# Seven block products in place of eight for values, feed-forward base and output projection of a gated attention block

## Chip, cores and metric

The kernel runs on one core of a Trainium2 chip. Its time is the device time in microseconds from launch to end, the median of several runs. The engines of a core work beside each other, each through its own queue in order: TensorE (PE in the profile; its weight loads PEld), VectorE (DVE), ScalarE (ACT), GpSimd (POOL), and SyncE (SP), which here issues nearly all transfers.

## Reference

Two batches of 1024 tokens with 512 features, all in fp32. D is 512, 32 heads of 16, 8 experts of rank 16 with the best 2 chosen.

```python
xn = layernorm(x)
q, k, v = xn @ Wq.T + bq, xn @ Wk.T + bk, xn @ Wv.T + bv
att = softmax(where(causal, q @ k.T / 4, -inf))       # per head
s = (att @ v) @ Wo.T + bo
base = xn @ W_base.T + b_base
route = top-2 of softmax(xn @ W_gate.T), normalized
delta = ((xn @ A.T) * route) @ B
g = silu(base + delta * SCALING)
out = x + s * g
```

## The kernel before

The work is cut into chunks (b, c) of 512 tokens, two batches by two chunks. Attention runs over *units* (b, oc, c): eight heads (oc) of one chunk. Each unit is a list of *steps*; 144 steps in all stand in `plan`. In a step n, TensorE computes the scores of four heads for 512 columns (`scores`, L923, tile `s`), ScalarE takes their exponential in two halves (L932, tile `pt`), VectorE multiplies the causal part by a mask (`masked`, L951; 83 of the 144 steps have one), and in the following step TensorE multiplies by the values (`values`, L967, tile `av`). The order in each engine's queue is: scores of step n, values of step n-1, masks of step n, then `fill(n)`.

`fill` is a planner that runs while the program is built. It holds every other piece of TensorE work as a `Task`, a generator that emits a piece and says what it cost. The unit of cost is `MM`, 0.853 us by the planner's own figure, for one group of eight matmuls with 512 columns (an fp32 matmul of a 128 by 128 block is issued as four strips of 32 columns, each in two passes). A task has a due step, an earliest step (`after`), buffers that it takes and frees (`room`), and a condition (`ready`). In each step the planner emits the ready tasks in order of due step, until the step has had its even share of what is left; work that is due is emitted whatever the share. Tasks without cost (layernorm, routing, loads) advance once in each step until they say `WAIT`. A list `later` holds the pieces of the softmax normalization that follow a unit by two to seven steps: the sums of the exponentials go to DRAM (`den`), come back spread over partitions (`dens`), their reciprocals go out (`back`) and in again (`avs`), all on SP's queue.

Three projections are the ones that the change touches. Each takes the normalized and transposed tokens `xnT` (or the attention output `oT`) as the matmul's left operand, 128 tokens at a time, and a weight that lies whole in SBUF (`wv_sb`, `wb_sb`, `wo_sb`, 1 MB each) as the right:

- values: `v_task` (L394), four groups a tile of 128 tokens, one VectorE addition of the bias (L402), into a tile of 17 columns a head;
- gate: `gate_task` (L498), four groups for the base and one more for the routed part in the same PSUM tile, one VectorE addition (L508), then tanh on ScalarE (L511) and two GpSimd operations (L512, L513);
- output: `out_task` (L598), four groups a tile, a VectorE addition (L607), two GpSimd operations (L608, L609) and the store. Each tile's x is loaded again (`load_x`, L88).

So a chunk costs 16 groups in each of the three, and 4 more for the routed part. The last chunk's output, at the end of the kernel, goes another way: `most_task`, `whole_task` and `rest_task` follow the last unit tile by tile, with x loaded by `bases_task` (L621) eight to nine steps before the end.

PSUM has two tiles for all of these projections (`ps_mm`), two for the scores and two for the attention output. `room` counts the SBUF buffers: one x chunk, three `xnT`, twelve `v` tiles, eight `g` tiles.

The transfers that matter in the order of SP's queue: a fill's own loads and stores as its tasks emit them, then what `later` emits, then those of tasks without cost. A transfer that has to wait for its operand keeps all behind it on that queue waiting.

Of the kernel before, what the change touches and what calls it, by code (L numbers as in the profile page):

```python
# [17 lines left out]
P = 128  # L18
# [41 lines left out]
def direct(ctx, tc, sound, x, wq, wk, wv, wo, wb, wa, wg, wB, bq, bk, bv, bo, bb, out):  # L60
# [22 lines left out]
    ps_av = ctx.enter_context(tc.tile_pool(name="ps_av", bufs=2, space=PSUM))  # L83


    def load_x(b, i):
        xt = sb.tile([P, D], F32, tag="xr", name=f"xr_{b}_{i}")
        nc.sync.dma_start(out=xt, in_=x[b, i * P : (i + 1) * P, :])  # L88
        return xt

    def chunk_tile(b, c):
        return sb.tile([P, TT, D], F32, tag="x", bufs=1, name=f"x_{b}_{c}")

# [5 lines left out]
    def load_w(src, cols, name, o0=0):  # L99
# [3 lines left out]
        )  # L103
        return t

    def load_b(src, name):
        t = cst.tile([P, D], F32, name=name)
        nc.sync.dma_start(out=t, in_=src.partition_broadcast(P))
        return t
# [3 lines left out]
    nc.scalar.dma_start(out=b_rows[KC : 2 * KC], in_=bk.rearrange("(kc p) -> kc p", p=P))  # L113
    wq_sb = [load_w(wq, P, "wq_sb0")]
    wk_sb = [load_w(wk, P, "wk_sb0")]
    wv_sb = load_w(wv, D, "wv_sb")
    bv_sb = load_b(bv, "bv_sb")
    for oc in range(1, KC):
        wq_sb.append(load_w(wq, P, f"wq_sb{oc}", oc * P))
        wk_sb.append(load_w(wk, P, f"wk_sb{oc}", oc * P))  # L120
    wag_sb = cst.tile([P, KC, ER + E], F32, name="wag_sb")
    wb_sb = cst.tile([P, KC, D], F32, name="wb_sb")
    wB_sb = cst.tile([P, D], F32, name="wB_sb")
    bb_sb = cst.tile([P, D], F32, name="bb_sb")
    wo_sb = cst.tile([P, KC, D], F32, name="wo_sb")
    bo_sb = cst.tile([P, D], F32, name="bo_sb")

    def load_rest():


        def by_rows(w):
            return w.rearrange("(kc p) o -> p kc o", p=P)

        for dst, src in (
            (wag_sb[:, :, 0:ER], by_rows(wa)),
            (wag_sb[:, :, ER:], by_rows(wg)),
            (wb_sb, by_rows(wb)),
            (wB_sb, wB),
            (bb_sb, bb.partition_broadcast(P)),
            (wo_sb, by_rows(wo)),  # L140
            (bo_sb, bo.partition_broadcast(P)),
        ):
            nc.sync.dma_start(out=dst, in_=src)
# [48 lines left out]
    def mm_tile(name):  # L192
        return ps_mm.tile([P, D], F32, tag="mm", name=name)
# [187 lines left out]
    def project(ps, b, i, w, stop=True):  # L381
        xnT, t = xnTs[b, i // TT], i % TT
        for k in range(KC):
# [7 lines left out]
            if k < KC - 1:  # L391
                yield

    def v_task(b, i):  # L394
        pv = mm_tile("pv")
        for _ in project(pv, b, i, wv_sb):
            yield MM
        v = sb.tile([P, VW], F32, tag="v", bufs=12, name=f"v_{b}_{i}")
        vh = v[:, 0 : H * VS].rearrange("p (h r) -> p h r", h=H)
        nc.gpsimd.memset(vh[:, :, HD : HD + 1], 1.0)  # L400
        nc.gpsimd.memset(v[:, H * VS : VW], 0.0)
        nc.vector.tensor_add(  # L402
            vh[:, :, 0:HD],
            pv.rearrange("p (h r) -> p h r", h=H),
            bv_sb.rearrange("p (h r) -> p h r", h=H),
        )
        vs[b, i] = v
        yield MM

    def routed_task(b, c):  # L410

# [83 lines left out]
        hls[b, c] = hl  # L495
        projected_at[b, c] = now[0]

    def gate_task(b, i):  # L498

        pb = mm_tile("pb")  # L500
        for _ in project(pb, b, i, wb_sb, stop=False):
            yield MM
        yield MM
        matmul(
            pb, lhsT=hwTs[b, i // TT][:, :, i % TT], rhs=wB_sb, start=False, stop=True
        )
        gt = sb.tile([P, D], F32, tag="g", bufs=8, name=f"g_{b}_{i}")
        nc.vector.tensor_add(gt, pb, bb_sb)  # L508

        sg = sb.tile([P, D], F32, tag="tmp", name="sg")  # L510
        nc.scalar.activation(sg, gt, AF.Tanh, scale=0.5)  # L511
        nc.gpsimd.tensor_scalar(sg, sg, 0.5, 0.5, ALU.mult, ALU.add)  # L512
        nc.gpsimd.tensor_tensor(gt, gt, sg, ALU.mult)  # L513
        gs[b, i] = gt
        yield MM

    def outputs(b, c):
        if (b, c) not in oTs:
            oTs[b, c] = sb.tile([P, KC, C], F32, tag="oT", name=f"oT_{b}_{c}")
# [69 lines left out]
    def project_out(po, b, c, t, k0, k1):  # L589
        for k in range(k0, k1):  # L590
            matmul(
                po, lhsT=oTs[b, c][:, k, t * P : t * P + P], rhs=wo_sb[:, k, :],
                start=k == k0, stop=k == k1 - 1,
            )
            if k < k1 - 1:
                yield

    def out_task(b, c):  # L598

        for t in range(TT):  # L600
            i = c * TT + t
            xt = load_x(b, i)
            po = mm_tile("po")
            for _ in project_out(po, b, c, t, 0, KC):
                yield MM
            y = sb.tile([P, D], F32, tag="tmp", name="y")
            nc.vector.tensor_add(y, po, bo_sb)  # L607
            nc.gpsimd.tensor_tensor(y, y, gs.pop((b, i)), ALU.mult)  # L608
            nc.gpsimd.tensor_tensor(y, y, xt, ALU.add)  # L609
            nc.sync.dma_start(out=out[b, i * P : (i + 1) * P, :], in_=y)  # L610
            yield MM

    def turn_last(b, c, t, turned):
        pt = mm_tile("pt_y")[:, 0:P]
# [1 line left out]
        nc.scalar.copy(oTs[b, c][:, KC - 1, t * P : t * P + P], pt)  # L616
        turned.append(t)

    bases = {}

    def bases_task(b, c):  # L621

        xt = chunk_tile(b, c)
        nc.sync.dma_start(
            out=xt, in_=x[b, c * C : (c + 1) * C].rearrange("(t p) d -> p t d", p=P)
        )
        for t in range(TT):
            bases[t] = xt[:, t]
        yield 0.0

    def finish_tile(b, c, t, po):
# [34 lines left out]
    def rest_task(b, c, t):  # L666

        turned = []
        last_in_range()
        yield lambda: turn_last(b, c, t, turned), TR  # L670
        while not turned:
            yield WAIT
        po = mm_tile("po")
        matmul(
            po, lhsT=oTs[b, c][:, KC - 1, t * P : t * P + P], rhs=wo_sb[:, KC - 1],
            start=True, stop=True,
        )
        pn = mm_tile("pn")[0:1, 0:NF]
        nc.tensor.matmul(pn, lhsT=ones, rhs=fine, start=True, stop=True)
        finish_tile(b, c, t, po)  # L680
        count = small.tile([1, 1], F32, tag="count", bufs=1, name="count")
        nc.vector.tensor_reduce(count, pn, AX.X, ALU.add)
        nc.vector.tensor_copy(sound, count)
        yield MM
# [54 lines left out]
        plan += [(u, s, n == 0, n == len(steps) - 1) for n, s in enumerate(steps)]  # L739


    room = {"x": 1, "xnT": 3, "qT": 3, "kT": 4, "v": 12, "hl": 1, "hwT": 2, "g": 8}
    users = {}

    class Task:
# [36 lines left out]
    def normalized(b, c):  # L782
        return sum(n < now[0] for n in posts.get((b, c), []))

    tasks = []
    for b in range(NB):
        for c in range(NC):
# [11 lines left out]
            for oc in range(KC):  # L799
                if oc or b or c:  # L800
# [3 lines left out]
                        ready=lambda u=units[units.index((b, oc, c)) - 1], t=turned_: u in qk_begun  # L804
                        and t(),
                    )
            for t in range(TT):
                use = s0 + ((5, 6, 13, 6) if c else (1, 3, 5, 3))[t]
                Task(use, v_task(b, c * TT + t), 4 * MM, takes={"v": 1}, uses=xn, ready=turned_)
            done = starts[b, KC - 1, c] + len(unit_steps(c))  # L810
            Task(
                done - 16, route_task(b, c), TT * KC * MM * (ER + E) / D, takes={"hl": 1}, uses=xn,
                ready=turned_,
            )
            Task(
                done - 14, routed_task(b, c), 0.0, takes={"hwT": 1}, frees={"hl": 1},
                ready=lambda u=(b, c): now[0] > projected_at.get(u, now[0]),
            )
            for t in range(TT):
                Task(  # L820
                    done - 11 + 2 * t, gate_task(b, c * TT + t), 5 * MM, takes={"g": 1},
                    uses=xn + [("hwT", b, c)], ready=lambda u=(b, c, "h"): now[0] > turned_at.get(u, now[0]) + 2,
                )
            if (b, c) != (NB - 1, NC - 1):
                by = min(len(plan) - 3, done + (21 if c else 17))
                Task(
                    by, out_task(b, c), 16 * MM, after=done + 2, frees={"g": TT},
                    ready=lambda b=b, c=c: normalized(b, c) == KC
                    and all((b, c * TT + t) in gs for t in range(TT)),
                )  # L830
            else:
                before = starts[b, KC - 1, c] + 2
                Task(len(plan) - 9, bases_task(b, c), 0.0, after=before, takes={"x": 1})
                Task(
                    len(plan) - 1, test_task(), 0.0, after=before,
                    ready=lambda: sum(len(x) for x in posts.values()) == len(units) - 1,
# [29 lines left out]
    def fill(n):  # L866
# [5 lines left out]
        for x in tasks:  # L872
            x.waiting = False

        begin = starts[units[-1]] + 2
        even = (total - spent) / max(1, len(plan) - n)
        if n == len(plan) - 1:
            even = 2 * MM
# [22 lines left out]
        for x in [x for x in later if x[0] <= n]:  # L901
            later.remove(x)
            x[1]()
        for x in [x for x in tasks if not x.cost and x.released(n)]:
            said = x.step()
            while said is not None and said is not WAIT:
                said = x.step()
        for _ in range(1 if active else 2):
            if late and (min(x[0] for x in late) <= n or not within):
                turn_late()  # L910
# [84 lines left out]
    for n, ((b, oc, c), _, _, is_last) in enumerate(plan):  # L995
        pts[n] = scores(n)
        if is_last:
            room["qT"] += 1
            room["kT"] += 2 if c == NC - 1 else 0
        if n > 0:  # L1000
            values(n - 1, pts.pop(n - 1))
            if plan[n - 1][0][1:] == (KC - 1, NC - 1) and plan[n - 1][3]:
                room["v"] += NC * TT
        masked(n, pts[n])
        fill(n)
    last = len(plan) - 1
# [468 lines left out]
```

## Time and profile before

| | |
|---|---|
| median of 3 runs | 628.74 us (628.66 to 628.77) |
| profiled execution | 628.33 us, span 626.6 us |
| granted TensorE clock, mean over the span | 0.997 |
| V: matmuls `pv`, busy | 59.9 us, 512 matmuls |
| base and routed part: `pb`, busy | 61.9 and 16.7 us, 512 and 128 matmuls |
| output: `po`, busy | 60.3 us, 512 matmuls |
| matmul `ph` (128x136), busy | 17.1 us, 512 matmuls |
| addition at L402, L508, L607, mean of one | 691, 689, 689 ns |
| exponential at L932, mean of one | 1021 ns |
| DMA: moved, mean rate | 29.61 MB, 47 GB/s |

The busy time of a group of matmuls counts overlapping instructions once. Matmuls are pipelined, so each is listed with 592 ns for 512 columns though one starts about every 107 ns; what counts is the distance from start to start, which the timeline shows. Each row of the profile's timeline gives the start, the length, the engine, the line, the operation, the tiles out<-in, the form and how many were merged; a bracket gives the idle time of the engine before it and what ended it.

### The profile page before, as it was taken

Reading aid. Unit: us, or ns where it says so; the run is one execution under the profiler, and the core shown is the slowest. Engines: PE = TensorE matmul, PEld = TensorE weight load, DVE = VectorE, ACT = ScalarE, POOL = GpSimd, SP = SyncE. Lnnn points to the kernel's source line nnn. Section 1 sums busy time; section 2 is a strip of 40 time slices with the busy share of each in tenths; the row PEclk is TensorE's granted clock in tenths of the full one; section 3 lists DMA queues with packets and bytes.
Section 4 is the critical chain, followed back from the end, with each engine's and each line's share of the span. In section 5 each row is a group of like instructions: output and inputs, shape, how many; then the busy total and the mean of one; then the engine's idle time right before and its main releaser. Section 6 shows DMA issues by size and latency. Waiting matters only on the chain.

```text
span 626.6 us, 15559 instructions
## 1 busy us (share of the span) xinstructions
PE 616.1 (98%) x6903; PEld 229.2 (37%) x6903; DVE 285.3 (46%) x570; ACT 298.0 (48%) x336; POOL 111.5 (18%) x132
## 2 busy tenths in 40 slices
PE   8999999999999999999999999999999999999995
PEld 7335322322334233332333322343233342245562
DVE  4454642423583546841545622324445637143533
ACT  2425345555555555554433554345545555435451
POOL 2101100010122001330351003300014200333260
PEclk9999999999999999999999999999999999999998
DMA  8913010003013040130120001200100000222001
GB/s 270 281 39 105 5 37 2 2 3 70 2 43 101 3 101 4 54 104 4 37 84 5 5 3 52 86 4 3 35 3 3 4 6 20 83 72 73 2 20 56
DMA packets 29467, 29.61 MB, mean 47 GB/s; under 512 B 6872, under 2 KB 19680, under 8 KB 29392
## 3 DMA queue, kind: packets, MB, share of 16 engines
q1 hardware_dynamic: 29376, 28.53, 15.2%
q8 instruction: 56, 0.92, 0.6%
q14 instruction: 19, 0.16, 0.1%
q10 hardware_dynamic: 16, 0.00, 0.0%
HBM read 19.65 MB, written 8.88 MB: 46 GB/s over the span
## 4 chain that ended last, share of the span: by engine, by line
PE 95%; DVE 2%; ACT 1%; DMA 0%; issue 0%; DVEq 0%
PE s L923 24%; PE av L967 22%; PE pb L198 10%; PE pv L198 9%; PE po L198 9%; PE pk L198 8%; PE pq L198 8%; PE ph L198 2%; PE pq_first L307 1%; DVE x L223 1%; ACT pt L932 0%; PE pk_first L307 0%; DMA x<-in_x_dram 0%; DVE st L212 0%; DVE pt L951 0%
## 5 line engine op out<-in xcount | busy, mean ns | idle before, releaser
L932 ACT ACTIVATE pt<-s 128x1024 f32<-128x1024 f32 x288 | 279.1, 1021 | 279.0 <-PE s L923 278.9
L951 DVE TENSOR_TENSOR pt<-pt,causal 128x256 f32<-128x256 f32 (+1 forms) x166 | 102.8, 631 | 145.2 <-ACT pt L932 145.1
L923 PE MATMUL s<-qT,kT 32*128 32x512 f32 (+3 forms) x1824 | 166.5, 464 | 0.3 <-ACT pt L932 0.2
L967 PE MATMUL av<-pt,v 128*32 128x512 f32 (+3 forms) x1824 | 155.0, 443 | 0.3 <-DVE pt L951 0.3
L923 PEld LDWEIGHTS s<-qT,kT 32*128 32x128 f32 x1824 | 72.7, 184 | 118.3 <-ACT pt L932 77.5
L967 PEld LDWEIGHTS av<-pt,v 128*32 128x32 f32 x1824 | 43.2, 109 | 90.0 <-issue 66.0
L198 PE MATMUL pb<-wb_sb,xnT 128*32 128x512 f32 x512 | 61.9, 592 | 0.0
L198 PE MATMUL po<-wo_sb,oT 128*32 128x512 f32 x512 | 60.3, 592 | 0.4 <-ACT oT L616 0.4
L198 PE MATMUL pv<-wv_sb,xnT 128*32 128x512 f32 x512 | 59.9, 592 | 0.0
L198 PE MATMUL pq<-xnT,wq_sb 128*32 128x512 f32 x480 | 57.0, 592 | 0.0
L198 PE MATMUL pk<-xnT,wk_sb 128*32 128x512 f32 x480 | 56.8, 592 | 0.0
L512 POOL TENSOR_SCALAR sg<-sg 128x512 f32<-128x512 f32 x16 | 10.9, 683 | 243.8 <-ACT sg L511 243.8
L546 POOL TENSOR_SCALAR avs<-avs,half 128x512 f32<-128x512 f32 x15 | 26.7, 1779 | 106.9 <-DMA den<-avs 85.0
L364 DVE TENSOR_SCALAR qT<-pq,b_sb,half 128x512 f32<-128x512 f32 x30 | 22.9, 805 | 42.0 <-PE pq L198 42.0
L608 POOL TENSOR_TENSOR y<-y,g 128x512 f32<-128x512 f32 x12 | 15.3, 1275 | 104.9 <-DVE y L607 104.9
L198 PEld LDWEIGHTS pv<-wv_sb,xnT 128*32 128x32 f32 x512 | 16.4, 110 | 34.0 <-issue 33.2
L198 PEld LDWEIGHTS po<-wo_sb,oT 128*32 128x32 f32 x512 | 16.2, 110 | 31.3 <-issue 30.2
L198 PEld LDWEIGHTS pk<-xnT,wk_sb 128*32 128x32 f32 x480 | 15.5, 110 | 32.3 <-issue 32.0
L198 PEld LDWEIGHTS pb<-wb_sb,xnT 128*32 128x32 f32 x512 | 16.6, 110 | 29.0 <-issue 28.1
L198 PEld LDWEIGHTS pq<-xnT,wq_sb 128*32 128x32 f32 x480 | 15.5, 110 | 30.8 <-issue 30.5
L377 DVE TENSOR_SCALAR kT<-pk,b_sb 128x512 f32<-128x512 f32 x15 | 11.2, 750 | 31.0 <-PE pk L198 30.8
L402 DVE TENSOR_TENSOR v<-pv,bv_sb 128x512 f32<-128x512 f32 x16 | 11.1, 691 | 30.5 <-PE pv L198 30.4
(92 smaller groups left out, 319.4 us busy)
## 6 DMA issues: line engine op xcount, KB each, us to landing
x<-in_x_dram SPq DMA_DIRECT2D x16, 256.0 KB
out_dram<-y SPq DMA_DIRECT2D x16, 256.0 KB
scr<-sq SPq DMA_DIRECT2D x6, 512.0 KB
xnT<-scr SPq DMA_DIRECT2D x24, 128.0 KB
xr<-in_x_dram SPq DMA_DIRECT2D x12, 256.0 KB
wq_sb<-in_wq_dram SPq DMA_DIRECT2D x4, 256.0 KB
wk_sb<-in_wk_dram SPq DMA_DIRECT2D x4, 256.0 KB
wv_sb<-in_wv_dram SPq DMA_DIRECT2D x1, 1024.0 KB
```

Of the source, the lines that this page charges most:

```text
L198: nc.tensor.matmul(o[j : j + 32], lhsT=lhsT[:, j : j + 32] if len(lhsT.shape) == 2 else lhsT[:, j // 32], rhs=rhs, start=start, stop=stop,)
L223: nc.vector.tensor_scalar(xt, xt, mv[:, t, 0:1], rstd[:, t : t + 1], ALU.subtract, ALU.mult)
L364: nc.vector.tensor_scalar(qT[:, par], pq, bq_sb[:, oc : oc + 1], half[:, par : par + 1], ALU.add, ALU.mult)
L377: nc.vector.tensor_scalar(kT, pk, bk_sb[:, oc : oc + 1], None, ALU.add)
L402: nc.vector.tensor_add(vh[:, :, 0:HD], pv.rearrange("p (h r) -> p h r", h=H), bv_sb.rearrange("p (h r) -> p h r", h=H),)
L512: nc.gpsimd.tensor_scalar(sg, sg, 0.5, 0.5, ALU.mult, ALU.add)
L546: nc.gpsimd.tensor_scalar(avs, avs, half[:, 1:2], None, ALU.mult)
L608: nc.gpsimd.tensor_tensor(y, y, gs.pop((b, i)), ALU.mult)
L923: nc.tensor.matmul(ss[s // 2][:, s % 2, col : col + w], lhsT=kT[rows, kt % TT * P : kt % TT * P + P], rhs=qTs[b, oc, c][rows, par, q0 : q0 ...
L932: nc.scalar.activation(pt[:, 2 * pair : 2 * pair + 2], ss[pair], AF.Exp, scale=0.25)
L951: nc.vector.tensor_tensor(d, d, mask, ALU.mult)
L967: nc.tensor.matmul(avs_now[par][32 * s : 32 * s + 32, q0 : q0 + w], lhsT=vs[b, kt][:, h * VS - HD * par : h * VS - HD * par + HP], rhs=pt[ ...
```

## The change

Each of ten projections of a chunk (three of V, four of the gate's base, three of the output) is computed by Winograd's form of Strassen's scheme over blocks of 256 by 256: seven products in place of eight, with four sums of token blocks and four sums of weight blocks. V of the first chunk and the output of the last stay as they were. The products go to PSUM one at a time and are added up on VectorE in the output tile.

The weight sums are made once in the kernel (`combine_task`) and stored in DRAM, and every block of weights, 256 KB, is loaded from DRAM for each product through six rotating buffers (`issue_parts`). The four token sums are made for each stage in a buffer that the weight sums use too (tag "sums", one buffer). The ten stages run one after the other in a fixed order. `room["xnT"]` starts at 2, since Wv takes the third buffer at first; later W_base, Wo and, at the end, x and Wo of the last chunk take such buffers. The output stage writes into the x chunk's buffer. Some due times move: routing and gate of the last chunk come earlier, and `begin`, up to which the planner spreads its work evenly, moves from two steps into the last unit to eight steps before the end.

```diff
-    wv_sb = load_w(wv, D, "wv_sb")
+    wv_sb = load_whole(wv, "wv")
...
-            (wb_sb, by_rows(wb)),
...
-            (wo_sb, by_rows(wo)),
...
+    BK = C // 2
+    PARTS = ("11", "t2", "21", "t3", "t1", "22", "t4")
+    stages = (
+        [("v", 0, 1), ("gate", 0, 0), ("gate", 0, 1), ("v", 1, 0), ("out", 0, 0), ("v", 1, 1)]
+        + [("out", 0, 1), ("gate", 1, 0), ("gate", 1, 1), ("out", 1, 0)]
+    )
+    NWP = 6
...
+    def combine_task(name, given=None):
+        src, bias = weights[name]
+        w = given or load_whole(src, f"w_{name}")
+        for _ in range(0 if given else 2):
+            yield WAIT
+        at = lambda i, j: w[:, 2 * i : 2 * i + 2, BK * j : BK * j + BK]
+        s = sb.tile([P, 4, 2, BK], F32, tag="sums", bufs=1, name="wsum")
+        nc.vector.tensor_tensor(s[:, 0], at(0, 1), at(0, 0), ALU.subtract)
+        nc.vector.tensor_tensor(s[:, 1], at(1, 1), s[:, 0], ALU.subtract)
+        yield WAIT
+        nc.vector.tensor_tensor(s[:, 2], at(1, 1), at(0, 1), ALU.subtract)
+        nc.vector.tensor_tensor(s[:, 3], at(1, 0), s[:, 1], ALU.subtract)
+        kept = dram.tile([P, 4, 2, BK], F32, tag=f"kept_{name}", bufs=1, name="kept")
+        nc.sync.dma_start(out=kept, in_=s)
+        d = cst.tile([P, BK], F32, name=f"bd_{name}")
+        nc.vector.tensor_tensor(d, bias[:, BK:D], bias[:, 0:BK], ALU.subtract)
+        combined[name], b_diff[name], kept_at[name] = kept, d, now[0]
+
+    def issue_parts():
+        while issued[0] < len(parts) and issued[0] - used[0] < NWP:
+            k, j = parts[issued[0]]
+            name = stages[k][0]
+            if now[0] < kept_at.get(name, now[0]) + 2:
+                return
+            part = PARTS[j]
+            w = sb.tile([P, 2, BK], F32, tag="wp", bufs=NWP, name=f"w{part}")
...
+            nc.sync.dma_start(out=w, in_=src)
+            places[k, j] = w
+            issued[0] += 1
...
+    def sums_task(k):
+        at = tokens(k)
+        s = sb.tile([P, 4, 2, BK], F32, tag="sums", bufs=1, name="asum")
+        nc.vector.tensor_tensor(s[:, 0], at(1, 0), at(1, 1), ALU.add)
+        nc.vector.tensor_tensor(s[:, 1], s[:, 0], at(0, 0), ALU.subtract)
+        sums[k], sums_at[k] = s, now[0]
+        yield WAIT
+        nc.vector.tensor_tensor(s[:, 2], at(0, 0), at(1, 0), ALU.subtract)
+        nc.vector.tensor_tensor(s[:, 3], at(0, 1), s[:, 1], ALU.subtract)
...
+        def product(name, a):
+            ps = mm_tile(name)
...
+            for i in range(2):
+                for kc in range(2):
+                    matmul(
+                        ps[:, i * BK : i * BK + BK],
+                        lhsT=a[:, kc, i * P : i * P + P],
+                        rhs=w[:, kc],
+                        start=i + kc == 0,
+                        stop=closes and i + kc == 2,
+                    )
+                if not i:
+                    yield MM
...
+        p1 = yield from product("p1", at(0, 0))
+        add(s11, p1, like(s11, bias[:, 0:BK]))
+        p6 = yield from product("p6", s[:, 1])
+        add(s12, p6, s11)
+        p2 = yield from product("p2", at(0, 1))
+        add(s11, p2, s11)
+        final(0, 0)
+        p7 = yield from product("p7", s[:, 2])
+        add(s21, p7, s12)
+        for o, t in ((s12, s12), (s22, s21)):
+            nc.vector.tensor_tensor(o, t, like(o, b_diff[name]), ALU.add)
+        p5 = yield from product("p5", s[:, 0])
+        add(s12, p5, s12)
+        add(s22, p5, s22)
...
+        p3 = yield from product("p3", s[:, 3])
+        add(s12, p3, s12)
+        final(0, 1)
...
+        p4 = yield from product("p4", at(1, 1))
+        add(s21, p4, s21)
+        final(1, 0)
...
+    def stage(task, what, due, cost, takes, uses, ready, frees=()):
+        k = stages.index(what)
+        Task(
+            due - 2, sums_task(k), 0.0, takes={"sums": 1},
+            ready=lambda: ended[0] == k and ready(),
+        )
+        Task(
+            due, task(k), cost, takes=takes, uses=uses, frees={"sums": 1, **dict(frees)},
+            ready=lambda: now[0] > sums_at.get(k, now[0]) and (k, 1) in places,
+        )
...
-        begin = starts[units[-1]] + 2
+        begin = len(plan) - 8
...
+        issue_parts()
```

`final` does what followed the bias addition before: nothing for V, tanh and two GpSimd operations for the gate, two GpSimd operations and the store of a block of 256 by 256 for the output, which also loads the next such block of x. For the gate, the routed part of a block is added by eight (in two passes, sixteen) further matmuls of 256 columns onto p2, p3 and p4, and in a tile of its own (`h`) for the fourth block. A V or output stage counts 14 MM for the planner where it was 16, a gate 18 where it was 20. The loads of W_base and Wo, which ran in the first 32 us, become 1 MB loads into `xnT` buffers ahead of `combine_task` for the gate (due at step 16) and the output (due at 17), and a load of the whole Wo next to x in `bases_task`.

## The prediction

> **What bounds the kernel now.** I read the page's busy shares and its chain first, then the waits of TensorE, then the order of time in single steps.
>
> ```profile
> span 626.6 us, 15559 instructions
> ...
> PE 616.1 (98%) x6903; PEld 229.2 (37%) x6903; DVE 285.3 (46%) x570; ACT 298.0 (48%) x336; POOL 111.5 (18%) x132
> ...
> PE 95%; DVE 2%; ACT 1%; DMA 0%; issue 0%; DVEq 0%
> ```
>
> TensorE is busy for 98% and is 95% of the chain. A busy TensorE may still wait, so the waits of PE (who, for whom: us, times, longest):
>
> ```profile
> PE warm L150 <- POOL ident masks.py:199: 1.4, 1, 1.4
> PE pt_x L296 <- DVE x L223: 1.0, 2, 0.7
> ...
> PE av L967 <- DVE pt L951: 0.3, 1, 0.3
> PE s L923 <- ACT pt L932: 0.2, 1, 0.2
> ```
>
> From the first score to the last step it waits for 0.5 us. So the time is the number of matmuls times their pitch, and one microsecond of matmul less is one less, as long as no new wait appears. The pitches come from the chain in order of time (start, length, matmuls) and, below it, the timeline of PE:
>
> ```profile
> 34.60 3.43 PE pq L198 x32
> ```
>
> ```profile
> 113.14 1.06 PE L967 MATMUL av<-pt,v 128*32 128x512 f32 x8
> 114.03 1.90 PE L198 MATMUL pb<-wb_sb,xnT 128*32 128x512 f32 x16
> 115.86 1.15 PE L923 MATMUL s<-qT,kT 32*128 32x256 f32 x16
> ...
> 120.72 1.07 PE L967 MATMUL av<-pt,v 128*32 128x256 f32 x16
> 121.61 1.04 PE L198 MATMUL pb<-wB_sb,hwT 128*32 128x512 f32 x8
> ```
>
> 32 projection matmuls of 512 columns take 3.43 us: 107.2 ns each, 0.858 us for a group of eight, which is one MM of the planner. Eight `av` matmuls of 512 columns take 114.03 - 113.14 = 0.89 us, sixteen of 256 columns 121.61 - 120.72 = 0.89 us (883 and 888 ns to the nanosecond). Half the columns is half the time. A usual step is 1.07 (s) + 0.89 (av) + 1.83 (two groups and the change of tile) = 3.79 us.
>
> **TensorE, the gain.** A stage (one of V, base or output for 512 tokens) is now 16 groups: 16 x 0.858 = 13.73 us. After the change it is 7 products of 32 matmuls, 128*32 by 128x256, the form of the `av` row. 883 ns is 8 x 107.2 and 25 ns for the tile change; (888 - 25)/16 = 53.9 ns; 7 x 32 x 53.9 ns = 12.07 us. Ten stages save 10 x 1.66 = 16.6 us. The routed part of the gate keeps its columns in pieces of 256 (+0.1), and ten stages of odd ends another 0.1: **-16.4 us**.
>
> A weight load takes 110 ns and now comes every 54 ns. Whether that hides is bounded by the narrowest projection: 56 `ph` matmuls of 136 columns with the same loads run from 48.86 to 50.60 in PE's timeline, 31.1 ns each, so loads hide at a closer pitch than is needed here.
>
> [...]
>
> **VectorE, what is added.** A stage has 4 evictions now; after it 4 sums over tokens, 7 product additions, one second use of p5 and two bias differences, 14 (gate 15, with h): 10 or 11 more in each, 104 in all, and 15 for the combined weights. At 0.69 us (the eviction at L508) that is 82 us: 285 becomes 367 us, 59% of the span. It is no bound by its mean. What it can do is deliver a causal mask late:
>
> ```profile
> 168.29 0.69 DVE L951 TENSOR_TENSOR pt<-pt,causal 128x512 f32<-128x512 f32 x1 [0.22 <-ACT pt L932]
> 168.90 0.69 DVE L212 BATCH_NORM_STATS2 st<-x 128x6 f32<-128x512 f32 x1
> ...
> 170.70 0.68 DVE L988 COPY oT<-av 128x512 f32<-128x512 f32 x1
> 171.30 0.68 DVE L990 COPY avs<-av 128x512 f32<-128x512 f32 x1
> 171.90 0.75 DVE L951 TENSOR_TENSOR pt<-pt,causal 128x256 f32<-128x256 f32 x2
> 172.57 0.68 DVE L508 TENSOR_TENSOR g<-pb,bb_sb 128x512 f32<-128x512 f32 x1
> 173.17 0.68 DVE L212 BATCH_NORM_STATS2 st<-x 128x6 f32<-128x512 f32 x1
> ```
>
> In a row, such operations come every 0.60 us (170.70, 171.30, 171.90). The step of the first line began at 165.08 (its `s` in PE's timeline): its masks end 3.9 us into the step, and `av` needs them at 3.79 + 1.07 = 4.86. So 0.9 us is to spare, and about 2 us of other work fits before the masks can begin (first exponential done at 2.2).
>
> **Where the covers end.** I followed the planner's rule with the new costs, due times and rooms. It still lays two groups, so one product, behind nearly every step, and each product has a step for its evictions. The trace's row durations, place by place:
>
> - Step 9. The first six weight parts are issued at the end of the fill before, behind `back<-rc` (67.81 in the trace, 0.33 long). A 256 KB transfer there needs 0.4 (issue), 0.45 to 0.84 to its first packet, 1.0 to 2.0 of data (xr of 304.46 ended at 306.98), 0.36 to its waiter: ready near 70.5. The fill starts at 68.60: **2.0** (0.5 to 3).
> - Steps 20 to 22. The combined weights and the token sums share one buffer, so gate (0,0)'s sums, emitted in the same fill, wait on VectorE's queue for the 1 MB store: 0.84 to its first packet, 2.8 at 380 GB/s (the densest stretch, 24 to 29 us), 0.36 behind. Issued at 116.9 by my times, done at 121.0; sums (1.3) and two wide masks (1.25) end at 123.5; `av` is due at 121.1. **2.4** (0 to 6, the upper end if the six parts ahead of it run at the 205 GB/s of the x load of 140.86).
> - Crowded masks. Worst is 56: masks end at 4.05, q pair 5.5, second sums 6.8, statistics of two tiles 8.6, which is 4.8 into step 57; its masks end at 6.05 against 4.86: 1.2, and 0.35 in 58. Likewise 0.4 at 36 and 0.7 at 79: **2.7** (0 to 6).
> - Steps 121 and 122 get no filler, since gate (1,1) waits for its routing; an empty step was 2.3 us long at 524.4, against 1.96 of matmuls: **0.5** (0 to 1.5).
> - The end. x and the whole Wo (2 MB, 5.6 us at 380 GB/s) now lie ahead of the last `avs<-back` on SP's queue; its normalisation ends 0.3 to 0.5 after the last tile's projection could start: **0.5** (0 to 4).
> - At nothing: 70 part loads (18 MB, 0.45 us of SP each). Six lie ahead, six steps or 23 us, against 2.5 us each. An issue that waits for the product that last read its buffer holds up `den`, `dens` and `back` behind it by less than a step, where they have two; SP's wait for GpSimd's product before an output store is there already. Without the cover each product would wait 2.5 us. The two 1 MB loads that leave the start were in nobody's way: TensorE waits for no weights there.
>
> Sum of the waits 8.1, so -16.4 + 8.1 = -8.3 us on the profiled execution's 628.33 (span 626.6 and 1.7 around it): 620.0. The median of the runs is 0.4 above it: **620.5 us**.
>
> **Rivals.**
> 1. *Clean*: the stores and parts land early, VectorE absorbs the rest, waits stay under 3 us: 613 to 615. For it: before, the same masks and layernorm shared a queue with 0.5 us of waits in all. Against: the shared buffer in steps 20 to 22 is a real order, not a matter of load.
> 2. *Slower: VectorE's queue becomes the bound.* 47 of the 83 masked steps follow a fill with sums, additions or combinations. At an average of 0.35 us late the gain is gone (47 x 0.35 = 16.4); at 0.5 us it is 23.5 and the time 628.7 - 16.4 + 23.5 = 636. For it: VectorE is stretched beside GpSimd (L215 took 0.17 us at 170.63 and 1.18 at 174.90, where GpSimd was at work). Against: 2 us of room and usually 0.6 to 1.8 of work.
> 3. *The saved columns don't pay*: 256 wide costs 62 ns in this mix, 7 x 32 x 62 = 13.9 a stage: 628 to 630 without waits. Against: the `av` and `ph` rows.
>
> **How the numbers follow.** Forecast (615 to 627.4) 0.54; clean (below 615) 0.17; slower by the queue 0.19; no saving 0.10, half of it within 0.2%. A measurement of this kernel can tell 0.2%, 1.3 us, from no change. Faster 0.54 + 0.17 = 0.71; same 0.05; slower 0.19 + 0.05 = 0.24. The likeliest's own range is 615 to 627; for 8 in 10 it reaches to 612 (clean, no waits) and to 633 (waits at their upper ends, 20.5 in all).
>
> **What would show it.** Right: matmuls of the product tiles near 54 ns start to start; VectorE near 365 us; PE's waits, now 0.5 us, near 8, the largest `av` for `pt` behind sums and one product for its weights near 70 us. Wrong: a pitch above 60 ns, part loads in PE's waits throughout, or masks late in most steps of the stages.

## The result, and the profile after

The changed kernel takes **633.23 us** (median of 10 runs, 630.75 to 635.70), the kernel before 628.70 in the same comparison (10 runs, 628.33 to 629.64). The ratio is 1.0071, its 95% interval 1.0053 to 1.0088: slower by 0.7%, where 620.5 and "faster" were forecast. The profiled execution took 632.31 us.

The page of the changed kernel, with the shares of its chain:

```profile
span 630.6 us, 18009 instructions
...
PE 610.1 (97%) x7991; PEld 273.6 (43%) x7991; DVE 370.6 (59%) x689; ACT 297.7 (47%) x336; POOL 112.3 (18%) x108
...
PE 73%; issue 9%; DVE 8%; DMA 5%; POOL 3%; ACT 1%; SPq 0%; DVEq 0%; POOLq 0%; ACTq 0%
```

The chain was 95% TensorE and is 73%. TensorE is still listed as busy for 97%, but part of that is long for another reason than work, as the clock will show. The waits of PE (for whom: us, times, longest), the three largest:

```profile
PE av L1183 <- DVE pt L1167: 6.2, 6, 3.2
PE p L195 <- DMA w<-in_wv_dram: 2.5, 1, 2.5
PE av L1183 <- DVE avs L1201: 1.9, 2, 1.5
```

10.6 us of waits where there were 0.5, all three kinds named in the forecast: masks behind sums, one product for its weights, the `avs` of the end.

To add up what each place costs, I took each of the 144 steps from one `s` to the next in PE's timeline and subtracted its matmuls (1.07 + 0.89, 0.858 for each old group or its share of a product, and 0.11 for the change of tile; the `ph` matmuls at 31.1 ns each). The matmuls sum to 589.6 us before and 572.5 after: **-17.1**. What lies above them is 5.9 us before and 26.7 after: **+20.8**. Together +3.7; the spans say 630.6 - 626.6 = 4.0. So the saving came in full, and the question is where the 20.8 us went.

| place | forecast | above its matmuls, after less before |
|---|---|---|
| step 9 (part loads) | 2.0 | 4.4 |
| steps 20 to 22 (shared buffer) | 2.4 | 5.1 |
| crowded masks (30, 37, 55 to 59, 76 to 80) | 2.7 | 5.7 (6.6 less 0.9 before) |
| steps 113 and 114 | 0 | 1.2 |
| steps 121 to 124 | 0.5 | -0.3 (1.6 less 1.9) |
| the end, 131 to 138 | 0.5 | 3.6 (4.8 less 1.15) |
| odd tenths elsewhere | 0 | 1.0 |

**Step 9 and its clock.** PE's timeline of the changed kernel around the first product:

```profile
71.57 3.42 PE L195 MATMUL p<-w,xnT 128*32 128x256 f32 x32 [2.51 <-DMA w<-in_wv_dram]
74.92 1.28 PE L1139 MATMUL s<-qT,kT 32*128 32x512 f32 x8
```

The product waits 2.51 us, as forecast (2.0, at most 3), but then its 32 matmuls take 3.42 us. Elsewhere the same product takes 1.9:

```profile
121.01 1.91 PE L195 MATMUL p<-w,xnT 128*32 128x256 f32 x32
122.85 1.15 PE L1139 MATMUL s<-qT,kT 32*128 32x256 f32 x16
127.23 2.09 PE L1183 MATMUL av<-pt,v 128*32 128x384 f32 x12 [3.23 <-DVE pt L1167]
```

From 121.01 to 122.85 the product costs 1.84 us, tile change included; two old groups cost 1.83. A stage has seven such products where it had eight pairs: the pitch of 53.9 ns held. The last line is step 22. Windows of time show why both places cost more than their waits (stretch and length; busy time of PE, PEld, DVE, ACT and POOL; then the granted clock, as a share of TensorE's full clock, DMA share, GB/s):

```profile
66.90:74.90 8.00, 5.49 (x68) 2.85 (x64) 3.74 (x8) 2.06 (x3) 0.00 (x0) 0.81 0.58 185
122.90:131.50 8.60, 5.37 (x68) 3.42 (x64) 5.60 (x9) 1.94 (x2) 0.00 (x0) 0.80 0.25 78
71.85:75.26 3.41, 3.41 (x36) 1.80 (x32) 0.22 (x1) 0.00 (x0) 0.00 (x0) 0.50 0.94 309
126.46:129.88 3.42, 2.65 (x24) 1.66 (x28) 3.42 (x7) 0.00 (x0) 0.00 (x0) 0.50 0.00 0
```

At both places the granted clock is 0.50 for 3.41 us: from 71.85, just after the first wait has ended (71.57), and from 126.46, 0.8 us before the second one ends (127.23). The first costs half of 3.41, 1.7 us, beside its wait (the product takes 1.5 us more than elsewhere, the scores behind it 0.14). At step 22 TensorE works for only 2.65 us of the stretch; the step is 4.9 us above its matmuls and `av` is 3.3 us late, so that 1.6 us are left for the clock. The waits of 1.0 to 1.5 us elsewhere are followed by no such stretch: the granted clock is 1.00 behind each of them. The mean clock of the ten runs is 0.987 to 0.993, 0.990 in the middle, against 0.997 before; 0.007 x 631 = 4.4 us is an estimate of what the half clock costs on average, a rough one, since the mean also counts the half clock behind the last step. It moves from run to run, and the times with it (630.75 us at 0.993, 634.22 to 635.70 us at 0.988), which is why this kernel's times spread over 5 us and those of the kernel before over 1.3.

The two stretches also show when the clock fell here. By the clock's records in this trace each lasts 3.413 us; 51.20 us of full clock lie between them and 494.93 from the second to the half clock behind the last step, 15 and 145 times 3.4133, so the changes of this trace lie on one grid of windows. In the window ahead of each of the two, TensorE is busy for less than 1 us of 3.41, and so stands still for 2.5:

```profile
68.44:71.85 3.41, 0.90 (x24) 0.41 (x20) 2.35 (x6) 1.71 (x3) 0.00 (x0) 1.00 0.50 156
123.05:126.46 3.41, 0.95 (x16) 0.52 (x13) 1.27 (x2) 1.94 (x2) 0.00 (x0) 1.00 0.59 183
```

**Step 22 and its order.** VectorE's timeline there:

```profile
120.53 0.42 DVE L447 TENSOR_TENSOR bd_out<-bo_sb 128x256 f32<-128x256 f32 x1
125.16 0.69 DVE L475 TENSOR_TENSOR asum<-xnT 128x512 f32<-128x512 f32 x1 [4.21 <-DMA kept<-wsum]
125.88 0.69 DVE L476 TENSOR_TENSOR asum<-asum,xnT 128x512 f32<-128x512 f32 x1
126.49 1.29 DVE L1167 TENSOR_TENSOR pt<-pt,causal 128x512 f32<-128x512 f32 x2
```

The token sums stand still for 4.21 us until the store has read the shared buffer, and the masks for `av` are queued behind them. The mechanism is the forecast's: issued at 120.64, the store let VectorE go on 4.5 us later, where 4.0 had been put down.

**The end.** VectorE in step 138:

```profile
591.25 0.01 DVE L757 LOAD_MASK_SELECT rb<-avs  x1 [0.72 <-DMA avs<-back]
...
592.67 1.48 DVE L876 TENSOR_SCALAR ok<-dens 128x480 f32<-128x480 f32 x1
...
595.45 0.48 DVE L1201 COPY avs<-av 128x128 f32<-128x128 f32 x2
```

`avs<-back` is late, as foreseen, but not for x and Wo alone: ahead of it SP issues an output store (586.01) that had to wait for GpSimd's product, done at 585.98. The normalisation then runs 591.25 to 592.7, three further operations of VectorE that begin at 592.67 lie ahead of the copy of `avs`, and `av` waits 1.48 us. Masks in this part are long as well: two narrow ones at 587.48 take 2.45 us together.

### The profile page after: what moved, and what is told of

Same layout as the page of the kernel before. It is cut to its first block, busy times and chain, and to the rows that moved or that the text cites. A ratio compares the mean times of both kernels' runs of the same rounds, so it can differ in the third digit from the quotient of the medians.

```text
span 630.6 us, 18009 instructions
## 1 busy us (share of the span) xinstructions
PE 610.1 (97%) x7991; PEld 273.6 (43%) x7991; DVE 370.6 (59%) x689; ACT 297.7 (47%) x336; POOL 112.3 (18%) x108
## 3 DMA queue, kind: packets, MB, share of 16 engines
q1 hardware_dynamic: 47328, 51.08, 27.6%
## 4 chain that ended last, share of the span: by engine, by line
PE 73%; issue 9%; DVE 8%; DMA 5%; POOL 3%; ACT 1%; SPq 0%; DVEq 0%; POOLq 0%; ACTq 0%
PE s L1139 18%; PE av L1183 18%; PE p L195 16%; PE pq L195 7%; PE pk L195 7%; PE pv L195 2%; PE po L195 2%; PE ph L195 2%; DVE pt L1167 1%; DMA w_out<-in_wo_dram 1%; DVE st L209 1%; DMA dens<-den 1%; POOL x L620 1%; DMA kept<-wsum 1%; POOL g L595 1%
## 5 line engine op out<-in xcount | busy, mean ns | idle before, releaser
L1183 PE MATMUL av<-pt,v 128*32 128x512 f32 (+3 forms) x1824 | 159.8, 445 | 8.1 <-DVE pt L1167 6.2
L1167 DVE TENSOR_TENSOR pt<-pt,causal 128x256 f32<-128x256 f32 (+1 forms) x166 | 111.1, 685 | 81.4 <-ACT pt L1148 81.0
L195 PE MATMUL p<-wt,asum 128*32 128x256 f32 x960 | 59.2, 381 | 0.0
L195 PEld LDWEIGHTS p<-wt,asum 128*32 128x32 f32 x960 | 32.2, 111 | 27.3 <-issue 10.5
L497 DVE TENSOR_TENSOR g<-p,g 128x512 f32<-128x512 f32 x28 | 18.9, 686 | 28.9 <-PE p L195 28.7
L619 POOL TENSOR_TENSOR x<-x,g 128x512 f32<-128x512 f32 x12 | 15.8, 1321 | 99.7 <-DMA den<-avs 45.7
L195 PE MATMUL p<-w,xnT 128*32 128x256 f32 x448 | 28.7, 395 | 2.5 <-DMA w<-in_wv_dram 2.5
L195 PEld LDWEIGHTS pk<-xnT,wk_sb 128*32 128x32 f32 x480 | 17.1, 110 | 31.8 <-issue 30.1
L497 DVE TENSOR_TENSOR v<-p,v 128x512 f32<-128x512 f32 x21 | 14.2, 690 | 21.2 <-PE p L195 21.2
L195 PEld LDWEIGHTS p<-w,xnT 128*32 128x32 f32 x448 | 15.4, 113 | 16.0 <-issue 7.7
L595 POOL TENSOR_TENSOR g<-g,sg 128x512 f32<-128x512 f32 x16 | 21.5, 1342 | 1.3
```

The costliest lines, as they stand in the source:

```text
L195: nc.tensor.matmul(o[j : j + 32], lhsT=lhsT[:, j : j + 32] if len(lhsT.shape) == 2 else lhsT[:, j // 32], rhs=rhs, start=start, stop=stop,)
L497: nc.vector.tensor_tensor(o, ps, t, ALU.add)
L595: nc.gpsimd.tensor_tensor(g(i, j), g(i, j), sg, ALU.mult)
L619: nc.gpsimd.tensor_tensor(y(i, j), y(i, j), g(i, j), ALU.mult)
L1167: nc.vector.tensor_tensor(d, d, mask, ALU.mult)
L1183: nc.tensor.matmul(avs_now[par][32 * s : 32 * s + 32, q0 : q0 + w], lhsT=vs[b, kt][:, h * VS - HD * par : h * VS - HD * par + HP], rhs=pt[ ...
```

## The experiments

In what follows, kernels 1, 2 and 3 are those of experiments 1, 2 and 3, and step numbers are those of the table. Theory A: the two long waits cost their length and a half-clock window behind, and the rest is VectorE's queue, stretched beside GpSimd. Theory B: the added VectorE work as such is the bound, so that removing the waits moves it little.

**1. First parts issued early**, ahead of the transfers that `later` emits:

```diff
+        if not used[0]:
+            issue_parts()
         for x in [x for x in later if x[0] <= n]:
```

> Edit: the first six weight parts are issued ahead of that fill's softmax transfers, and nothing else is moved. Theory (the loss sits in few places, and a wait of over 2 us also halves the TensorE clock for a while): step 9 goes from 8.0 to 3.8 us, the 2.5 us wait for the first part and the 1.7 us of half clock behind it both vanish; the median falls from 633.2 to about 629, the mean granted clock rises by about 0.003. Rival (VectorE's queue is the bound, a wait removed comes back later): step 9 is shorter, but the later steps lengthen, and the median stays within 1.5 us of 633.2.

Measured 628.68 us (10 runs, 626.70 to 631.08), ratio 1.0002 (0.9989 to 1.0015). Step 9 is back at 3.79 us; step 22 keeps its 5.2 us above the matmuls. The wait of 2.5 us was worth 4.6 us of median time. The runs follow their clocks: 626.70 at 0.996, 631.08 at 0.987.

**2. Weight sums in the loaded weight's own buffer**, so that the token sums have theirs free; the order of work is as it was, and the sums are stored in four transfers where it was one:

```diff
-        s = sb.tile([P, 4, 2, BK], F32, tag="sums", bufs=1, name="wsum")
-        nc.vector.tensor_tensor(s[:, 0], at(0, 1), at(0, 0), ALU.subtract)
+        nc.vector.tensor_tensor(at(0, 0), at(0, 1), at(0, 0), ALU.subtract)
...
-        nc.sync.dma_start(out=kept, in_=s)
+        for n, (i, j) in enumerate(((0, 0), (1, 1), (0, 1), (1, 0))):
+            nc.sync.dma_start(out=kept[:, n], in_=at(i, j))
```

> Edit: the weight sums are made in place in the buffer of the loaded weight, so that the token sums of gate (0,0) no longer wait for the 1 MB store. Theory: step 22 goes from 8.7 to about 3.8 us (3.2 of wait, 1.7 of half clock), the median from 633.2 to about 628.5, the clock rises by about 0.003. Rival (VectorE is simply late there, the store only happens to lie beside it): step 22 stays above 6 us and the median within 1.5 us of 633.2.

Measured 625.52 us (4 runs, 625.38 to 625.69), ratio 0.9949 (0.9933 to 0.9966): 7.7 less than the changed kernel and 3 us less than expected. Step 22 is back at 3.8 us. Step 9 still waits, a little less long; PE's timeline:

```profile
71.21 1.93 PE L195 MATMUL p<-w,xnT 128*32 128x256 f32 x32 [2.36 <-DMA w<-in_wv_dram]
```

and the window of that step:

```profile
66.60:73.20 6.60, 4.24 (x72) 2.40 (x72) 3.74 (x9) 2.06 (x3) 0.00 (x0) 1.00 0.49 138
```

2.36 us of waiting, no half clock after it, and the step costs 2.6 instead of 4.4. So some 1.8 us of the 7.7 are step 9's, though the edit is for step 22. The place of the wait on the grid fits this. The only half clock of this kernel's trace, behind its last step, begins at 619.10; counted back from there in 161 steps of the 3.4133 us of the changed kernel's trace, a window ends at 69.55, in the midst of the wait (an estimate: no half clock shows the grid here in the middle):

```profile
66.14:69.55 3.41, 2.71 (x40) 1.14 (x32) 2.64 (x7) 1.67 (x2) 0.00 (x0) 1.00 0.09 9
69.55:72.96 3.41, 1.75 (x32) 1.13 (x32) 1.09 (x2) 0.39 (x2) 0.00 (x0) 1.00 0.79 234
```

The wait is split: TensorE stands still for 0.7 us in one window and 1.66 in the next, and neither is followed by half clock.

**3. Both.**

> Both edits. Theory: the gains add, since the two places are far apart: 5.7 us of waits and the half-clock windows, which in the ten runs cost 4.5 us on average by their mean clock, so about 623 us, faster than before the change (628.7); and the spread of the runs, 5 us for the changed kernel, falls below 1.5 us, with the mean clock at 0.996 as in the kernel before. Rival (the clock falls for the busier VectorE or the streamed weights, not for the waits): the clock stays near 0.990, the spread stays near 5 us, and the time is 627 or more.

Measured 623.23 us (4 runs, 623.03 to 623.42), ratio 0.9911 (0.9894 to 0.9927); span 621.6, profiled clock 0.998. The runs lie within 0.4 us. Edits 1 and 2 take 4.6 and 7.7 alone and 10.0 together: less than 12.3, because in kernel 2 the wait of step 9 brought no half clock in the profile (the other runs, at 0.996 and 0.997, agree), and so left only some 2.6 us there for edit 1 to take (2.3 by the medians). The changed kernel is slower only through these two places; theory B, with nothing but the queue, falls.

**4. The half clock by itself.** In the kernel before, at step 28, a stall on VectorE ahead of the masks and nothing else (9 additions; the second kernel has 7):

```diff
+        if n == 28:
+            slow = sb.tile([P, D], F32, tag="tmp", name="slow")
+            nc.vector.memset(slow, 0.0)
+            for _ in range(9):
+                nc.vector.tensor_tensor(slow, slow, slow, ALU.add)
         masked(n, pts[n])
```

> The kernel before the change, with a memset and nine additions of a scratch tile put on VectorE's queue ahead of the masks of step 28, nothing else changed: the values product of that step is about 3.3 us late. Theory (a wait of this length halves the clock in one or two windows of 3.4 us): the time rises by 3.3 us and 0 to 3.4 us more, about 633 us, the runs spread over 2 us or more, and the time of a run follows its mean clock. Rival (the half clock of the changed kernel has another cause): 632.0 us in every run, spread as before (0.3 us, one stray), clock 0.997.

> The kernel before with two additions fewer in the delay than in b_stall9, where the wait was 3.3 us and the half clock cost 3.4 more. The wait becomes about 2.1 us. Theory (the clock looks at windows of 3.41 us that run free, and halves when TensorE was mostly idle in one): a wait of 2.1 us leaves 1.3 us of work in any window and costs itself alone, 630.8 us, clock 0.996. Rival (any wait over a microsecond or two halves it): 632.5 or more.

With 9 additions `av` waits 3.97 us. The window of the step:

```profile
142.30:152.90 10.60, 6.63 (x48) 2.63 (x44) 6.66 (x11) 1.94 (x2) 0.00 (x0) 0.68 0.41 93
```

The step is 6.75 us above its matmuls: 4.0 by the wait and some 2.7 by the clock, not 3.3 and 3.4 as the second expectation has it. The clock is at half for 6.83 us, two windows, of which the first begins 1.9 us before the wait ends:

```profile
142.12:145.53 3.41, 1.34 (x12) 0.31 (x8) 3.24 (x6) 1.94 (x2) 0.00 (x0) 1.00 1.03 247
145.53:148.94 3.41, 1.51 (x12) 0.64 (x16) 2.41 (x4) 0.00 (x0) 0.00 (x0) 0.50 0.29 54
148.94:152.35 3.41, 3.41 (x26) 1.63 (x18) 0.64 (x1) 0.00 (x0) 0.00 (x0) 0.50 0.00 0
```

TensorE stands still for 2.07 us in the first window and 1.9 in the second, and each is followed by one at half clock. The times agree: 635.98 us (4 runs, 635.67 to 636.54), ratio 1.0117, 7.2 above the kernel before. With 7 additions the wait was 2.5 (2.1 was expected):

```profile
142.70:151.40 8.70, 6.17 (x48) 2.36 (x44) 4.89 (x9) 1.94 (x2) 0.00 (x0) 0.80 0.53 116
```

In the profile one half-clock window of 3.41 us; the four runs are 631.56 to 633.71, median 632.43, ratio 1.0055 (1.0038 to 1.0072), with mean clocks of 0.994 to 0.997, so that, going by the clocks, only some of them lost it. The profiled step is 4.9 us above its matmuls: 2.6 late, 1.7 for the window, and 0.6 that no row explains. A wait of 2.1 us was not made, so this run doesn't decide between theory and rival: 630.8 is missed, and the median lies at the rival's 632.5. A wait alone, with no block products anywhere, brought the half clock in both profiles, 6.83 and 3.41 us of it. The spread of the 9-addition kernel was smaller than expected: its mean clock is 0.992 in all four runs, so, going by the clocks, the wait of 4 us lost two windows each time.

**5. GpSimd out of the way.** Kernel 3 without GpSimd's operations in the gate and the output:

```diff
-            nc.gpsimd.tensor_scalar(sg, sg, 0.5, 0.5, ALU.mult, ALU.add)
-            nc.gpsimd.tensor_tensor(g(i, j), g(i, j), sg, ALU.mult)
...
-            nc.gpsimd.tensor_tensor(y(i, j), y(i, j), g(i, j), ALU.mult)
-            nc.gpsimd.tensor_tensor(y(i, j), y(i, j), xts[i, j], ALU.add)
```

> e3 with GpSimd's two operations of every gate block and of every output block of the ten stages left out, so the gate and the residual are not applied there; all transfers, products and VectorE additions stay. What is left of e3's excess over its matmuls (621.6 against 609.5 by the sum, 12.1 us) lies in steps 30, 37, 55 to 59, 76 to 80, 113, 114, 121 to 123 and 131 to 138. Theory (VectorE's SBUF operations stand still while GpSimd works, masks stretched by 1.06 us): steps 30, 76 to 80, 113, 114 and 131 to 136 come back to 3.8 us, about 6 us in all, while 55 to 59 (layernorm and sums in one queue) stay: 617 us. Rival (it is the number of VectorE's operations): under 2 us, 621.5 or more.

Measured 615.84 us (one run), 7.4 below kernel 3 though TensorE's and ScalarE's work is the same and VectorE has the same 689 instructions. Steps 30, 55 to 57, 76 to 78, 113 and 131 lose their excess; 37, 58, 59, 80 and 121 to 123 keep all or most of it, 114 keeps half, and 138 falls from 1.74 to 0.79. The rival falls; of the theory's places, 55 to 57 came back, which were expected to stay, and 80 stayed, which was expected to come back. The timelines show one reason. VectorE in kernel 3, two masks in each of the first two lines:

```profile
326.52 2.78 DVE L1169 TENSOR_TENSOR pt<-pt,causal 128x512 f32<-128x512 f32 x2 [0.82 <-ACT pt L1150]
...
330.32 3.17 DVE L1169 TENSOR_TENSOR pt<-pt,causal 128x512 f32<-128x512 f32 x2 [0.16 <-ACT pt L1150]
...
334.96 1.76 DVE L751 SCALAR_TENSOR_TENSOR oT<-oT,half,avs 128x512 f32<-128x512 f32 x1 [0.86 <-POOL avs L748]
```

GpSimd in kernel 3 at the same time:

```profile
329.98 1.29 POOL L619 TENSOR_TENSOR x<-x,g 128x512 f32<-128x512 f32 x1 [1.23 <-DVE x L497]
331.35 1.60 POOL L620 TENSOR_TENSOR x<-x,xr 128x512 f32<-128x512 f32 x1
```

VectorE at the same place without them:

```profile
324.32 0.69 DVE L1165 TENSOR_TENSOR pt<-pt,causal 128x512 f32<-128x512 f32 x1 [0.81 <-ACT pt L1146]
325.24 0.69 DVE L1165 TENSOR_TENSOR pt<-pt,causal 128x512 f32<-128x512 f32 x1 [0.22 <-ACT pt L1146]
```

A pair of masks takes 3.17 us beside GpSimd; one alone takes 0.69. The run takes away more than this stretching: at 334.96 VectorE also waits 0.86 us for `avs`, which GpSimd made after the products, and at the end SP's stores no longer wait for GpSimd. The 7.4 us are the price of GpSimd's operations by all three ways, which were not separated. Over the whole trace VectorE's time above the usual length of each form is 28.1 us in kernel 3, 3.8 here and 16.5 before the change. What was stretched in these traces are operations with both inputs in SBUF (masks and token sums, 0.69 us and up to about 1.1 more each) and, more rarely, the normalisation at L220 (0.54 us, once 1.29); the product additions, which read PSUM, stay at 0.68 to 0.69 in the midst of it. In the changed kernel's trace all 39 rows of VectorE that take over 0.06 us more than the median of their form lie beside a row of GpSimd, and all 84 product additions take 0.66 to 0.69 us, nine of them with GpSimd at work for over 0.3 us. Why the one kind stands still and the other doesn't, no run shows.

**6. The same left out of the kernel before**, as a control:

> Control: the kernel before with the same GpSimd operations left out (two for every gate tile, two for every output tile of the first three chunks), so the gate and the residual are not applied there. There GpSimd stretches VectorE by 16.5 us in all too. Theory (a stretched mask costs only where the queue behind it has no room left, which the change used up): under 1 us less, 628 us, where the same removal in e3 took 7.5. Rival (the stretch costs the same in both, and the change only inherited it): 4 us less or more, 624.5 or below.

Measured 627.93 us (8 runs, 627.32 to 628.22) against 628.60, ratio 0.9986 (0.9975 to 0.9998): 0.7 us. The same GpSimd work costs 7.4 us after the change and 0.7 before it, though VectorE stood still for 16.5 us then too. In the profile the gain lies in one place, step 59, where 0.88 us above the matmuls go to nothing. That VectorE's queue had room elsewhere, at 46% of the span against 59%, fits this; it was not tested by itself.

**7. Token sums left out** of kernel 3:

```diff
-        s = sb.tile([P, 4, 2, BK], F32, tag="sums", bufs=1, name="asum")
-        nc.vector.tensor_tensor(s[:, 0], at(1, 0), at(1, 1), ALU.add)
...
+        sums[k], sums_at[k] = (at(0, 0), at(0, 1), at(1, 0), at(1, 1)), now[0]
```

> e3 with the four token sums of every stage left out: 40 VectorE operations of 128x512 less, the products take plain blocks, so V, gate and output come out otherwise. Theory (places, with GpSimd beside the masks): 56 to 59, 78 and 131 become shorter, about 3.5 us: 619.7 us. Rival (the count of VectorE's operations is the cost, 0.35 us late in each of 47 masked steps by 10 to 11 operations a stage): four tenths of all 12 us go, 618.5 or less, spread over all stages.

Measured 618.79 us (one run), 4.4 below kernel 3: between the two expectations, so the time doesn't tell them apart. The places speak for the theory: steps 57, 58, 80 and 131 lose their excess, 55, 76 to 78 and 113 keep it, and nothing is spread over all stages. The costs of experiments 5 and 7 overlap (57 and 131 are in both, 58 in part) and can't be added.

**8. Kernel 3 with the last chunk's work moved**: its routing twelve steps earlier, and the layernorm of (1, 1) six.

```diff
-                    s0 - 4, layernorm_task(b, c), 0.0, after=s0 - (40 if c == 0 else 30) if b else -9,
+                    s0 - 4, layernorm_task(b, c), 0.0, after=s0 - (40 if c == 0 else 36) if b else -9,
...
-                done - (16 if (b, c) != (NB - 1, NC - 1) else 28), route_task(b, c), TT * KC * MM * (ER + E) / D, takes={"hl": 1}, uses=xn,
+                done - (16 if (b, c) != (NB - 1, NC - 1) else 40), route_task(b, c), TT * KC * MM * (ER + E) / D, takes={"hl": 1}, uses=xn,
...
-                done - (14 if (b, c) != (NB - 1, NC - 1) else 26), routed_task(b, c), 0.0, takes={"hwT": 1}, frees={"hl": 1},
+                done - (14 if (b, c) != (NB - 1, NC - 1) else 38), routed_task(b, c), 0.0, takes={"hwT": 1}, frees={"hl": 1},
```

> e3 with three due times moved: routing of the last chunk 12 steps earlier, layernorm of chunk (1,1) 6 steps earlier. Theory: steps 121 and 122 are filled again and step 129 no longer has six groups (1.5 us, and 1.0 at 131), and 55 to 59 lose their crowd (2.5 of 3.3 us): 618.5 us. Rival (VectorE is full, the crowd only moves): 622.5 or more, with new long steps at 48 to 55 or 105 to 110.

Measured 619.44 us (4 runs, 619.13 to 620.77), ratio 0.9859 (0.9843 to 0.9876): the fastest that still computes the whole block, 1.4% under the kernel before. Steps 57 to 59 and 121 to 123 lose their excess; 113 to 116 rise from 1.2 to 1.95, and 76 to 80 and most of the end stay as in kernel 3.

## Why the prediction was wrong, point by point

- **TensorE, -16.4**: right; -17.1 by the steps. Neither the pitch (53.9 ns) nor the hidden weight loads (110 to 113 ns each by the means of their groups in the changed kernel's trace) were off, so the rival "the saved columns don't pay" falls.
- **VectorE, 367 us**: 370.6, with 27.6 us above the usual length of each form in it.
- **Step 9, 2.0, and steps 20 to 22, 2.4**: the mechanisms and the waits were right (2.5 and 3.2 us, inside their bounds); what they cost was 4.4 and 5.1. **This is the first failed step**: each wait was added at its own length, and nothing was put down for the clock after it. The sum lacked 1.7 + 1.6 = 3.3 us for the clock in the profile, and some 4.4 us on average by the estimate above; the other 1.8 us of the two misses are longer waits and a step 20 of 0.2. The trace of before held no wait of that length in its middle, so it didn't show this. Experiments 1 to 3 show that the two places cost 10.0 us together, and experiment 4 that a wait alone did it there, with 0.50 for 6.83 us.
- **Crowded masks, 2.7, and 113 and 114, nothing**: 5.7 and 1.2. **The second failed step**: the working of step 56 sums VectorE's rows at their undisturbed 0.69 us, while a row beside GpSimd (L215, 0.17 and 1.18 us) was named only as support for a rival and entered no term. Experiment 5 shows that GpSimd's operations cost 7.4 us, at 55 to 57, 76 to 78, 113 and the end for the most part, and experiment 6 that the change made them cost that. What the forecast did name held: it counts a late mask at its own step and the table at the next, where `av` waits, so its 0.4 at 36, 1.2 at 57, 0.35 at 58 and 0.7 at 79 stand against 0.5 at 37, 1.9 at 58, 0.45 at 59 and 0.6 at 80, together 3.5 us for 2.7. The other 3.1 us of the row, at 30, 55 to 57 and 76 to 78, stood in no term, and experiment 5 takes them away.
- **The end, 0.5**: 3.6, within its 0 to 4. Two things were left out: masks and sums stretched by GpSimd at 131, and in 138 an output store waiting for GpSimd ahead of `avs<-back`, with three other operations of VectorE next in line.
- **Empty steps, 0.5**: -0.3, since before had its own stall at 123 and 124, which went.
- **Part loads at nothing**: right; PE's waits name a weight only once, in step 9.

The misses are -0.7 (TensorE), 2.4, 2.7, 3.0, 1.2, 3.1, -0.8 and 1.0 of odd tenths: 11.9 of the 12.3 us between 620.0 and the profiled 632.3. Of the rivals, *slower by VectorE's queue* had the right sign and the wrong weight: crowded masks, 113 and 114 and the end cost 10.5 us in some 18 steps, not 0.35 us in 47, and with the two long waits gone the kernel is 0.9% faster than before with that queue untouched. *Clean* at 613 to 615 is nearly what kernel 3 gives without GpSimd (615.84).

37, 58, 59 and 80, which stay late without GpSimd, are the forecast's own places; 58 and 80 lose their excess without the token sums (experiment 7) and 58 and 59 with the layernorm moved (experiment 8), so there VectorE's own work is the crowd. What is left open: 37 was not tried by itself, nor how the 3.6 us of the end divide between the transfers and the masks.

## What to carry to other kernels

A wait of TensorE cost more than its length in these kernels, which otherwise hardly let it rest: where 1.9 us or more of standing still fell into one window of 3.41 us, the next ran at a clock of 0.50, which is 1.7 us when it is full of work, and the changed kernel's times spread over 5 us where those before spread over 1.3. In a kernel like these, allow for that where a new wait may put as much into one window. Before work is added to VectorE, lay GpSimd's timeline beside it and cost operations with two SBUF inputs by their stretched rows (a mask up to 1.79 us), not by their best ones (0.69). A buffer that a store reads from shouldn't be the one that the next step on the busy queue writes to: here its own buffer took 5.5 us off between kernels 1 and 3, and 7.7 where it also spared step 9's half clock.

## What was not expected of the hardware

In the middle of these kernels the half clock came in whole windows of 3.41 us, and whether a wait met one went with how much of it fell into one window of the grid. In the profiles of all runs here, a window in the middle of a kernel in which TensorE stood still for 1.9 us or more (1.9 and 2.07 with 9 additions, 2.46 and 2.51 in the changed kernel, 2.5 with 7 additions, 3.0 in kernel 1) was followed by one at half clock, and none with 1.66 or less was; what happens in between, no run shows. So the wait of 2.36 us brought none, split as it was; those of 2.5 brought one in step 9's profile and, going by the mean clocks, in part of the executions of the 7-addition stall; those of 3.0 and 3.2 brought one; and 3.97 brought two in a row, 6.83 us.
